# Local deformable attention: dense weights by one read per tile and one write per head, values by quarters, tokens loaded two chunks ahead

## The chip, the cores and the metric

The kernel runs on one core of a Trainium2 chip. The metric is the device time of one execution in microseconds (us). A core has TensorE (PE, whose weight loads are shown as PEld), VectorE (DVE), ScalarE (ACT) and GpSimd (POOL), and SyncE (SP), which issues transfers (DMAs); in this kernel ACT issues some too. Each engine runs its own instructions in the order in which they were put on its queue, and waits at an instruction until what it needs has come. L750 is line 750 of the kernel before.

## The reference, cut to what matters

The program is four layers; the change touches the first one's convolution. For every pixel of a 64 x 64 image, nine taps of four head groups (dilations 1, 3, 5, 7) are moved by learned offsets; keys and values are sampled there bilinearly, weighted by a mask, and attended over the nine taps.

```python
qkv = x @ w_qkv + b_qkv
qkv = conv2d(qkv.transpose(0, 3, 1, 2), w_dw, padding=1, groups=3 * c) + b_dw[None, :, None, None]
...
mask = jax.nn.sigmoid(conv1x1(pconv(q_img, pconv_mask_w), w_mask, b_mask))
for i in range(G):
    off = conv1x1(pconv(q_img, pconv_off_w[i]), w_off[i], b_off[i])
    dil = 2 * i + 1
    k_list.append(deform_sample(kv[0, :, i], off, mask, dil, dil * PAD))
    v_list.append(deform_sample(kv[1, :, i], off, mask, dil, dil * PAD))
...
attn = jax.nn.softmax(jnp.einsum('bgnc,bgckn->bgnk', qf, ks_), axis=-1)
out = jnp.einsum('bgnk,bgckn->bgnc', attn, vs_)
out = out.transpose(0, 2, 1, 3).reshape(b, h, w, c)
return out @ w_proj + b_proj
```

The layer adds its input to this: x + conv(norm(x)).

## The kernel before

`deformable_project` computes queries, keys, values and offsets of the four images (batches) and stores them to DRAM (qd, kd, vd, od). Where no offset is larger than one pixel, `deformable_near` does the rest. It needs no gather: every sample lies within one pixel of its tap, so a sample is a sum over a 3 x 3 neighbourhood with bilinear "hat" weights.

The near stage works on tiles of 128 pixels (two image rows), 32 to a batch, 128 in all; four tiles are a chunk, 32 chunks. A loop over T goes through the tiles, and the second half of a tile's work comes LAG = 14 tiles after the first. For tile or chunk:

- *Products* (`product`, L750): PE multiplies the tile's queries, laid out on POOL (qm, L721), with a band of keys from kpad, and ACT copies the result to `band` (`copy_products`, L760). band has two buffers per group, one chunk each.
- *Hats* (POOL, per chunk): from the offsets (of), `hats` makes the weights (L694 to L698), multiplies them by the mask (L702), and `hat_products` makes H, 3 x 3 weights of each tap (L708, four instructions of 324 elements). H has three buffers.
- *Attention* (DVE, per chunk, `attention`): within its tile a pixel's band starts at its own place; copies under a mask (`bit`) shift it there, first by one row (L768), then by 4, 2 and 1 columns (L771). Then band times H (L775), the sum (L782), the maximum, the exponential on ACT (L798), and `spread` (L799 to L818), which multiplies softmax weights and H into rows A.
- *Dense rows*: SP writes A to DRAM (`write`, L826: 16 transfers a chunk, one for each group and quarter of the partitions, since the row shift r is in the address), and every tile reads it back skewed (`read_dense`, L837: four transfers, two on SP, two on ACT), so that D holds a dense row of weights per pixel over a window of pixels. The DRAM buffers dd are zeroed once at the stage's start.
- *Values*: PE transposes D (L868), ACT copies to dt (L870), and PE multiplies with blocks of values (`weigh`, L888), each loaded by four transfers (`value_block`, L849).
- *Output* (per chunk): ACT copies the sum (oT, L900), SP loads the chunk's tokens xg (L904), POOL adds the bias (L905), PE projects (L911), ACT copies o (L913), POOL adds it to xg (L914), and SP stores the tokens (L920). xg has two buffers.

The order on PE is written out: `block` makes each of transpose, product, projection and weigh follow the one before (`issue_after`), and what stands in `behind` follows the last block. On the other engines a scheduler places the instructions by its own estimate of when they can run, so an engine's order may differ from the order of the calls; transfers are issued from the engine that the call names, in that engine's order.

## Time and profile before

| | |
|---|---|
| median of 3 runs | 7,705.08 us (7,700.91 to 7,719.4) |
| profiled execution | 7,690.3 us |
| its span | 7,688.3 us |
| mean granted TensorE clock | 0.892 |
| `deformable_project` | 0 to 671 us |
| near stage, start until the first steady chunks | 671 to 778 us |
| near stage, remainder | 778 to about 1,835 us |
| the other layers | about 1,835 to 7,688 us |

The page's 40 slices of 192 us each show the busy tenths of each engine; the near stage is in slices 4 to 9. The busy time of each engine by stage, in us:

| window | PE | PEld | DVE | ACT | POOL | clock | DMA share | GB/s |
|---|---|---|---|---|---|---|---|---|
| 0 to 671 | 566 | 251 | 123 | 209 | 8 | 0.94 | 0.44 | 105 |
| 671 to 778 | 51 | 38 | 68 | 16 | 81 | 0.66 | 0.72 | 218 |
| 778 to 1,835 | 788 | 661 | 669 | 357 | 392 | 0.83 | 0.71 | 201 |
| 1,835 to 7,688 | 5,117 | 2,592 | 3,961 | 2,109 | 1,261 | 0.90 | 0.12 | 32 |

### The profile page before, as it was taken

The numbers are of one execution on the slowest core, as the hardware profiler recorded it, in microseconds if no ns is written. First come the engines' busy times: TensorE is split into PE (matmuls) and PEld (weight loads), VectorE is DVE, ScalarE is ACT, GpSimd is POOL, SyncE is SP. The second block draws the span as 40 slices with busy tenths as digits, with TensorE's granted clock in tenths as the row PEclk, the third lists the DMA queues.
The fourth block names the chain that finished last, engine by engine and source line by source line (L and its number), as shares of the span: only waits on it lengthen the run. The fifth ranks groups of instructions, "written<-read, shape, count | busy, mean of one in ns | idle before, by whom it ended". The sixth has DMA issues, their size and how long they took to land. (4 is left out here: it accounts for less than half of the span.)

```text
span 7688.3 us, 157708 instructions
## 1 busy us (share of the span) xinstructions
PE 6522.7 (85%) x63791; PEld 3542.4 (46%) x63791; DVE 4821.5 (63%) x11178; ACT 2690.3 (35%) x6141; POOL 1741.4 (23%) x1634
## 2 busy tenths in 40 slices
PE   7995777775688868989989999798898997997989
PEld 3343666663455644345555555445225234242244
DVE  2113766764277554858856656674785875867877
ACT  3331333333234313611146555565104013031056
POOL 0003444320001100035532221154012112120135
PEclk9997887887799889999999988798897997988989
DMA  4436677775400022030100000001111111111101
GB/s 121 98 87 179 187 209 205 213 199 172 143 4 1 2 60 48 10 117 22 27 12 10 9 10 6 9 1 30 39 25 49 26 33 40 25 35 38 25 23 31
DMA packets 678781, 495.59 MB, mean 64 GB/s; under 512 B 302326, under 2 KB 594104, under 8 KB 674200
## 3 DMA queue, kind: packets, MB, share of 16 engines
q1 hardware_dynamic: 480910, 354.59, 17.0%
q10 hardware_dynamic: 197130, 130.77, 6.2%
q8 instruction: 509, 8.34, 0.5%
q14 instruction: 232, 1.90, 0.1%
HBM read 335.28 MB, written 149.75 MB: 63 GB/s over the span
## 5 line engine op out<-in xcount | busy, mean ns | idle before, releaser
L2476 DVE TENSOR_TENSOR t<-S,q 128x1536 f32<-128x1536 f32 (+3 forms) x608 | 1156.9, 1948 | 123.2 <-PE S L2464 117.9
L2464 PE MATMUL S<-R,L 32*128 32x512 f32 x4096 | 734.6, 651 | 90.3 <-DMA R<-wd 78.9
L2492 PE MATMUL acc<-t,sum 128*32 128x512 f32 x4096 | 639.5, 608 | 0.0
L750 PE MATMUL S<-kpad,qm 32*64 32x240 f32 (+3 forms) x8192 | 403.4, 421 | 216.0 <-ACT band L760 97.5
L2178 PE MATMUL pe<-ew,yT 128*128 128x512 f32 x1024 | 479.4, 603 | 27.4 <-DVE xs L2184 24.5
L1777 PE MATMUL acc<-w,attT 128*64 128x264 f32 x4096 | 486.3, 391 | 10.4 <-DVE w L1773 10.4
L2464 PEld LDWEIGHTS S<-R,L 32*128 32x128 f32 x4096 | 200.6, 186 | 611.4 <-issue 280.4
L2498 ACT COPY agg<-acc 128x512 f32<-128x512 f32 x32 | 18.8, 586 | 1194.0 <-DMA L<-pd 626.7
L750 PEld LDWEIGHTS S<-kpad,qm 32*64 32x64 f32 x8192 | 299.9, 156 | 271.5 <-issue 136.9
L1770 POOL TENSOR_TENSOR w<-xtl,ei 128x528 f32<-128x528 f32 x256 | 332.1, 1319 | 309.6 <-ACT ei L1769 204.5
L2184 DVE SCALAR_TENSOR_TENSOR xs<-pe,gate,xs 128x128 f32<-128x128 f32 x1024 | 332.5, 345 | 96.5 <-PE pe L2178 79.8
L1773 DVE TENSOR_TENSOR w<-xtl,pe 128x1056 f32<-128x1056 f32 x256 | 320.3, 1251 | 100.3 <-ACT ei L1769 89.4
L1777 PEld LDWEIGHTS acc<-w,attT 128*64 128x64 f32 x4096 | 284.0, 137 | 197.5 <-DVE w L1774 38.0
L2187 ACT ACTIVATE sc<-pe,gate 128x128 f32<-128x128 f32 x1024 | 291.3, 374 | 202.2 <-PE pe L2178 194.1
L514 PE MATMUL dw<-pad,diag 32*32 32x512 f32 x6912 | 310.4, 614 | 12.9 <-issue 7.0
L2507 POOL TENSOR_TENSOR o<-o,bf 128x512 f32<-128x512 f32 x32 | 40.7, 1271 | 1229.4 <-ACT o L2506 1229.4
L760 ACT COPY band<-S 128x144 f32<-128x144 f32 (+3 forms) x512 | 136.0, 351 | 480.4 <-DMA D<-dd 152.3
L2492 PEld LDWEIGHTS acc<-t,sum 128*32 128x32 f32 x4096 | 92.7, 108 | 458.4 <-issue 436.1
L2178 PEld LDWEIGHTS pe<-ew,yT 128*128 128x128 f32 x1024 | 185.6, 193 | 234.3 <-issue 151.4
L768 DVE COPY_PREDICATED band<-bit,band 128x432 f32<-128x432 int32 (+3 forms) x128 | 107.5, 895 | 270.0 <-ACT band L760 264.2
L868 PE MATMUL pt<-ident,D 128*128 128x128 f32 x1536 | 243.0, 315 | 29.2 <-DMA D<-dd 15.2
L771 DVE COPY_PREDICATED band<-bit,band 128x288 f32<-128x288 int32 (+11 forms) x384 | 243.0, 742 | 0.0
(520 smaller groups left out, 13065.8 us busy)
## 6 DMA issues: line engine op xcount, KB each, us to landing
vb<-vd SPq DMA_DIRECT2D x272, 256.0 KB
D<-dd ACTq DMA_DIRECT2D x128, 192.0 KB
D<-dd SPq DMA_DIRECT2D x128, 168.0 KB
D<-dd ACTq DMA_DIRECT2D x128, 144.0 KB
w<-in_e_weight_dram ACTq DMA_DIRECT2D x16, 1024.0 KB
w<-in_e_weight_dram SPq DMA_DIRECT2D x16, 1024.0 KB
wd<-s SPq DMA_DIRECT2D x32, 512.0 KB
D<-dd SPq DMA_DIRECT2D x128, 120.0 KB
```

What stands on the lines that cost most here:

```text
L514: nc.tensor.matmul(acc[g][32 * c : 32 * c + 32], diag[r, j, tap, :], pads[j][r, y0 : y0 + 8, tx : tx + 64], start=(tap == 0), stop=(tap == 8),
L750: ins = nc.tensor.matmul(acc[g][64 * h : 64 * h + 64].rearrange("p (a s) c -> p a s c", a=3), qm[rows, h, m, :], keys, start=(m == 0), sto ...
L771: nc.vector.copy_predicated(rows(0, [[CW[g], 3], [1, n]]), bit[:, :, :, i : i + 1].to_broadcast([128, 12, 3, n]), rows(s, [[CW[g], 3], [1, ...
L1770: nc.gpsimd.tensor_tensor(w2[:, 2:4], xt[:, 2:4, 0:2], window(ei, 0, [[0, 2], [0, 2], [1, 132]]), op=ALU.mult)
L1773: nc.vector.tensor_tensor(w1, xt[:, :, 1:3], window(pe, 0, [[0, 4], [0, 2], [1, 132]]), op=ALU.mult)
L1777: nc.tensor.matmul(acc[b // 2][64 * (b % 2) : 64 * (b % 2) + 64], attT[:, b // 2, hp, 64 * (b % 2) : 64 * (b % 2) + 64], src[:, b].rearran ...
L2178: nc.tensor.matmul(pe[h].rearrange("p e c -> p (e c)"), yT[:, 128 * t : 128 * t + 128], ew[:, 4 * h : 4 * h + 4, :].rearrange("p e c -> p ...
L2184: nc.vector.scalar_tensor_tensor(xt, pe[0][:, e, :], gate[:, t, e : e + 1], xt, op0=ALU.mult, op1=ALU.add)
L2187: nc.scalar.activation(sc[:, e, j, :], pe[1][:, e, :], AF.Copy, scale=gate[:, t, 4 + e : 5 + e])
L2464: nc.tensor.matmul(S[:, j, :], Ls[n % 2][r, ag, :], Rs[n % 2][r, ag].rearrange("p x y -> p (x y)"), start=True, stop=True)
L2476: nc.vector.tensor_tensor(t[:, j0:j1].rearrange("p u (x y) -> p u x y", x=8), S[:, j0:j1].rearrange("p u (x y) -> p u x y", x=8), qf[:, q0 ...
L2492: nc.tensor.matmul(acc[0][32 * h : 32 * h + 32, :], sum4, t[:, j, :], start=(u < 4), stop=(u >= 60))
```

## The change

- The dense rows: one buffer dd per chunk (three in turn) holds all four groups, with a row of 4 x 4 x 384 elements and 12 more (before: a buffer per group, of 240 to 384 elements a tile). `write` makes one transfer per group, four a chunk; `read_dense` one per tile, all on SP, and it covers the full 384 elements of each group.
- The row shift r is no longer in the address: hats along y have four rows instead of three, and `rows_of_hats` puts a pixel's three weights into rows 0 to 2 or 1 to 3 by its bit (`row`). So H, prod and t0 have 12 elements a tap instead of 9, A is filled over four rows, and the copies under a mask by one row (L768) are left out; those by 4, 2 and 1 columns run over all 48 rows. H has two buffers instead of three, dt three instead of four.
- The zero fill: three buffers, each by four transfers of 768 KB and a small one, all on ACT; only one tile of D is set to zero first.
- Values: `deformable_project` copies the values of each batch from vd into vq, rearranged by quarters (four transfers from DRAM to DRAM on SP). `value_block` is then one transfer.
- Offsets, queries, keys and tokens are loaded by ACT instead of SP. The tokens' load is called at the second tile of a chunk's last part, instead of after its fourth. Bias and tokens are added behind the projection's copy, next to the add of o.
- The hats are called three tiles earlier and the H products one; the offsets' loads three. A store is called two tiles after its add at the earliest.

In the changed program as it is built, these instructions stand so on POOL and ACT (steady part, one chunk, in order; a slash separates):

- POOL: add of o (chunk c) / add of the bias (chunk c+2) / two query copies / two H products / half a query copy / H / half a query copy / H / hats (four instructions) / their rows (seven) / a query copy / add of o (chunk c+1).
- ACT: tokens' load (chunk c+2) / band copies of the last tile of a chunk / dt / band copies / dt / exp / band copies / queries' load / oT / dt / offsets' load / band copies / copy of o / dt / tokens' load (chunk c+3).
- SP, per chunk: four writes of A / values / read of D / store of tokens / read of D / values / two reads of D.

```diff
+        vq = [dr.tile([32, 84, 4, 128], F32, tag=f"vq{b}", name=f"vq{b}") for b in range(4)]
...
+            for q in range(4):
+                nc.sync.dma_start(vq[b][:, :, q, :], vd[b][16 * q : 16 * q + 32])
...
-    PP = [12 * (15 + w) for w in W]
+    ROW = 4 * 4 * 384 + 12
...
+        row = wp.tile([128, 1], F32, tag="row", name="row")
+        nc.vector.tensor_copy(row, bit[:, 0, 0, 3:4])
...
-        dd = [[dr.tile([128, 4 * PP[g] + 12], F32, tag=f"dd{i}{g}", name=f"dd{i}{g}") for g in range(4)] for i in range(2)]
+        dd = [dr.tile([128, ROW], F32, tag=f"dd{i}", name=f"dd{i}") for i in range(3)]
 
         dense = [wp.tile([128, 4, 384], F32, tag=f"D{i}", name=f"D{i}") for i in range(4)]
-        for t in dense:
-            nc.gpsimd.memset(t, 0.0)
-        for i in range(2):
-            for g in range(4):
-                zero = dense[g].rearrange("p t n -> p (t n)")
-                eng = (nc.sync, nc.scalar)[g % 2]
-                eng.dma_start(dd[i][g][:, 0 : 4 * PP[g]], zero[:, 0 : 4 * PP[g]])
-                eng.dma_start(dd[i][g][:, 4 * PP[g] : 4 * PP[g] + 12], zero[:, 0:12])
-        Hs, bands, outs, vblocks, logits, ofs, hat_of, queries = {}, {}, {}, {}, {}, {}, {}, {}
-        accs, lefts, project, stores = {}, {}, [], []
-        last = [None]
+        nc.gpsimd.memset(dense[0], 0.0)
+        zero = dense[0].rearrange("p g n -> p (g n)")
+        for d in dd:
+            for t in range(4):
+                nc.scalar.dma_start(d[:, 1536 * t : 1536 * t + 1536], zero)
+            nc.scalar.dma_start(d[:, 6144:ROW], zero[:, 0:12])
+        Hs, bands, outs, vblocks, logits, ofs, hat_of, hy_of, queries = {}, {}, {}, {}, {}, {}, {}, {}, {}
+        accs, lefts, inputs, project, stores = {}, {}, {}, [], []
+        last, now = [None], [0]
...
-            nc.sync.dma_start(ofs[c], od[b][:, 4 * c8 : 4 * c8 + 4, :])
+            nc.scalar.dma_start(ofs[c], od[b][:, 4 * c8 : 4 * c8 + 4, :])
...
-            of = ofs.pop(c)
+            of = ofs[c]
...
-            mk = sm.tile([128, 3, 4, 3], F32, tag="mk", name="mk")
-            nc.gpsimd.tensor_copy(mk, window(of, 72, [[3, 3], [81, 4], [1, 3]]))
+        def rows_of_hats(c):
+            of, hat = ofs.pop(c), hat_of[c]
+            mk = sm.tile([128, 2, 36], F32, tag="mk", name="mk")
+            at = lambda i: window(mk, 36 * i, [[0, 4], [1, 36], [0, 3]])
+            nc.gpsimd.tensor_copy(mk[:, 0].rearrange("p (a t n) -> p a t n", a=3, t=4), window(of, 72, [[3, 3], [81, 4], [1, 3]]))
+            nc.gpsimd.tensor_scalar(mk[:, 1], mk[:, 0], row, None, op0=ALU.mult)
+            nc.gpsimd.tensor_tensor(mk[:, 0], mk[:, 0], mk[:, 1], op=ALU.subtract)
             hy = hat[:, 0:4].rearrange("p s a t n i -> p s (a t n) i")
-            nc.gpsimd.tensor_tensor(hy, hy, window(mk, 0, [[0, 4], [1, 36], [0, 3]]), op=ALU.mult)
-            Hs[c] = sm.tile([128, 4, 36, 9], F32, tag="H", name="H", bufs=3)
+            h4 = hy_of[c] = sm.tile([128, 4, 36, 4], F32, tag="hy", name="hy", bufs=1)
+            nc.gpsimd.tensor_tensor(h4[:, :, :, 0:3], hy, at(0), op=ALU.mult)
+            nc.gpsimd.tensor_tensor(hy, hy, at(1), op=ALU.mult)
+            nc.gpsimd.tensor_tensor(h4[:, :, :, 1:3], h4[:, :, :, 1:3], hy[:, :, :, 0:2], op=ALU.add)
+            nc.gpsimd.tensor_copy(h4[:, :, :, 3], hy[:, :, :, 2])
 
         def hat_products(c, groups):
-            H, hat = Hs[c], hat_of[c]
+            if 0 in groups:
+                Hs[c] = sm.tile([128, 4, 36, 12], F32, tag="H", name="H")
+            H, hat, h4 = Hs[c], hat_of[c], hy_of[c]
             for g in groups:
                 nc.gpsimd.tensor_tensor(
-                    H[:, g].rearrange("p n (a c) -> p n a c", a=3), window(hat, 108 * g, [[3, 36], [1, 3], [0, 3]]),
-                    window(hat, 108 * (4 + g), [[3, 36], [0, 3], [1, 3]]), op=ALU.mult,
+                    H[:, g].rearrange("p n (a c) -> p n a c", a=4), window(h4, 144 * g, [[4, 36], [1, 4], [0, 3]]),
+                    window(hat, 108 * (4 + g), [[3, 36], [0, 4], [1, 3]]), op=ALU.mult,
...
-            nc.sync.dma_start(
+            nc.scalar.dma_start(
...
-            nc.sync.dma_start(queries[n], qd[b].rearrange("p (y x) -> p y x", x=64)[:, 8 * h : 8 * h + 8, :])
+            nc.scalar.dma_start(queries[n], qd[b].rearrange("p (y x) -> p y x", x=64)[:, 8 * h : 8 * h + 8, :])
...
-            prod = sm.tile([128, 4, 36, 9], F32, tag="prod", name="prod", bufs=1)
+            prod = sm.tile([128, 4, 36, 12], F32, tag="prod", name="prod", bufs=1)
...
-                rows = lambda off, dims: window(band[g], off, [[4 * CW[g], 12]] + dims)
-                n = 3 * CW[g]
-                nc.vector.copy_predicated(rows(0, [[1, n]]), bit[:, 0, :, 3:4].to_broadcast([128, 12, n]), rows(CW[g], [[1, n]]))
+                flat = band[g].rearrange("p a t s c -> p (a t s) c")
                 for i, s in enumerate((4, 2, 1)):
                     n = W[g] + s - 1
-                    nc.vector.copy_predicated(
-                        rows(0, [[CW[g], 3], [1, n]]), bit[:, :, :, i : i + 1].to_broadcast([128, 12, 3, n]), rows(s, [[CW[g], 3], [1, n]])
-                    )
+                    nc.vector.copy_predicated(flat[:, :, 0:n], bit[:, 0, :, i : i + 1].to_broadcast([128, 48, n]), flat[:, :, s : s + n])
                 for tx in range(3):
                     nc.vector.tensor_tensor(
-                        window(prod, 324 * g + 9 * tx, [[27, 12], [3, 3], [1, 3]]),
-                        window(band[g], DIL[g] * tx, [[4 * CW[g], 12], [CW[g], 3], [1, 3]]),
-                        window(H, 324 * g + 9 * tx, [[27, 12], [3, 3], [1, 3]]), op=ALU.mult,
+                        window(prod, 432 * g + 12 * tx, [[36, 12], [3, 4], [1, 3]]),
+                        window(band[g], DIL[g] * tx, [[4 * CW[g], 12], [CW[g], 4], [1, 3]]),
+                        window(H, 432 * g + 12 * tx, [[36, 12], [3, 4], [1, 3]]), op=ALU.mult,
...
-                        window(A[g], ty, [[12 * DIL[g], 12], [3, 3], [12, 3]]), window(H, 324 * g + 108 * ty, [[9, 12], [3, 3], [1, 3]]),
-                        window(lg, 36 * g + 12 * ty, [[1, 12], [0, 3], [0, 3]]), op=ALU.mult,
+                        window(A[g], ty, [[12 * DIL[g], 12], [3, 4], [12, 3]]), window(H, 432 * g + 144 * ty, [[12, 12], [3, 4], [1, 3]]),
+                        window(lg, 36 * g + 12 * ty, [[1, 12], [0, 4], [0, 3]]), op=ALU.mult,
...
-            t0 = sm.tile([128, 36, 9], F32, tag="t0", name="t0", bufs=1)
-            nc.vector.tensor_tensor(t0, H[:, 0], window(lg, 0, [[1, 36], [0, 9]]), op=ALU.mult)
+            t0 = sm.tile([128, 36, 12], F32, tag="t0", name="t0", bufs=1)
+            nc.vector.tensor_tensor(t0, H[:, 0], window(lg, 0, [[1, 36], [0, 12]]), op=ALU.mult)
             for ty in range(3):
-                a0 = lambda m0, n: window(A[0], 12 * m0 + ty, [[60, 4], [12, n], [3, 3]])
-                tap = lambda tx, s0, n: window(t0, 108 * ty + 9 * tx + s0, [[27, 4], [1, n], [3, 3]])
+                a0 = lambda m0, n: window(A[0], 12 * m0 + ty, [[60, 4], [12, n], [3, 4]])
+                tap = lambda tx, s0, n: window(t0, 144 * ty + 12 * tx + s0, [[36, 4], [1, n], [3, 4]])
...
-            A = As[c % 2]
-            for g in (1, 2, 3, 0):
-                d, P = dd[c % 2][g], PP[g]
-                for j in range(4):
-                    r = j % 2
-                    nc.sync.dma_start(
-                        bass.AP(
-                            d.tensor, d.offset + 32 * j * (4 * P + 12) + 3 * r, [[4 * P + 12, 32], [P, 4], [1, 12 * W[g]]]
-                        ),
-                        A[g][32 * j : 32 * j + 32, :, 0 : W[g]].rearrange("p t c s a -> p t (c s a)"),
-                    )
+            for g, d in enumerate(DIL):
+                m = dd[c % 3]
+                nc.sync.dma_start(
+                    bass.AP(m.tensor, m.offset + 384 * g + 12 * (7 - d), [[ROW, 128], [1536, 4], [1, 12 * W[g]]]),
+                    As[c % 2][g][:, :, 0 : W[g]].rearrange("p t c s a -> p t (c s a)"),
+                )
 
         def read_dense(T):
             c, t = divmod(T, 4)
-            for g, d in enumerate(DIL):
-                m, P = dd[c % 2][g], PP[g]
-                (nc.sync, nc.scalar)[g % 2].dma_start(
-                    dense[t][:, g, 12 * (7 - d) : 12 * (7 - d) + P],
-                    bass.AP(m.tensor, m.offset + t * P, [[16 * (4 * P + 12), 8], [4 * P, 16], [1, P]]),
-                )
+            m = dd[c % 3]
+            nc.sync.dma_start(
+                dense[t].rearrange("p g n -> p (g n)"), bass.AP(m.tensor, m.offset + 1536 * t, [[16 * ROW, 8], [ROW - 12, 16], [1, 1536]])
+            )
...
-            d = vd[b]
-            for q in range(4):
-                nc.sync.dma_start(
-                    t[:, q].rearrange("p s c -> p (s c)"),
-                    bass.AP(d.tensor, d.offset + 16 * q * 10752 + 4 * kb * 128, [[10752, 32], [128, 4], [1, 512]]),
-                )
+            d = vq[b]
+            nc.sync.dma_start(
+                t.rearrange("p s q c -> p (s q c)"), bass.AP(d.tensor, d.offset + 4 * kb * 512, [[84 * 512, 32], [512, 4], [1, 2048]])
+            )
...
+            if T % 4 == 1:
+                inputs[0] = sm.tile([128, 4, 128], F32, tag="xg", name="xg")
+                nc.scalar.dma_start(inputs[0], tokens(x, b, i - 1, 4))
...
-                dt = sm.tile([128, 4, 128], F32, tag="dt", name="dt", bufs=4)
+                dt = sm.tile([128, 4, 128], F32, tag="dt", name="dt", bufs=3)
...
-                                quarter(outs[0][32 * g : 32 * g + 32, T % 4, :], q), vblocks[b, kb][:, q, si, 32 * g : 32 * g + 32],
+                                quarter(outs[0][32 * g : 32 * g + 32, T % 4, :], q), vblocks[b, kb][:, si, q, 32 * g : 32 * g + 32],
...
-                xg = sm.tile([128, 4, 128], F32, tag="xg", name="xg")
-                nc.sync.dma_start(xg, tokens(x, b, 4 * c, 4))
-                nc.gpsimd.tensor_tensor(xg, xg, bpj.to_broadcast([128, 4, 128]), op=ALU.add)
+                xg = inputs[0]
...
+            nc.gpsimd.tensor_tensor(xg, xg, bpj.to_broadcast([128, 4, 128]), op=ALU.add)
...
-            stores.append((b, c, xg))
+            stores.append((now[0], b, c, xg))
...
-        def store():
-            for b, c, xg in stores:
+        def store(some):
+            for o in some:
+                _, b, c, xg = o
                 nc.sync.dma_start(tokens(y, b, 4 * c, 4), xg)
-            stores.clear()
+                stores.remove(o)
...
+        offsets(1)
         products(0)
+        hats(0)
+        rows_of_hats(0)
         for T in range(128 + LAG):
+            now[0] = T
             with behind():
                 step(T, -1, products)
-                step(T, -2, offsets, 4)
-                step(T, 0, hats, 4)
-                step(T, 1, lambda c: hat_products(c, (0, 1)), 4)
-                step(T, 2, lambda c: hat_products(c, (2, 3)), 4)
+                step(T, -5, offsets, 4)
+                step(T, 0, lambda c: hat_products(c, (0, 1)), 4)
+                step(T, 1, lambda c: hat_products(c, (2, 3)), 4)
+                step(T, -2, hats, 4)
+                step(T, -1, rows_of_hats, 4)
...
-            late = list(stores)
+            late = [o for o in stores if o[0] <= T - 2]
...
-                if late:
-                    store()
+                store(late)
```

More of the change, by code (lines that the diff above doesn't have):

```diff
@@ L386, in stage_deformable @@
         od = [dr.tile([128, 32, 81], F32, tag=f"od{b}", name=f"od{b}") for b in range(4)]
-        far = deformable_project(k, fp, x, qd, kd, vd, od, w_qkv, b_qkv, w_dw, b_dw, pconv, w_offT, b_off)
+        vq = [dr.tile([32, 84, 4, 128], F32, tag=f"vq{b}", name=f"vq{b}") for b in range(4)]
+        far = deformable_project(k, fp, x, qd, kd, vd, vq, od, w_qkv, b_qkv, w_dw, b_dw, pconv, w_offT, b_off)
         with tc.If(far > 0) as branch:
@@ L390, in stage_deformable, with deformable_project @@
         with branch.Else():
-            deformable_near(k, dr, x, y, qd, kd, vd, od, masks, w_proj, b_proj)
-def deformable_project(k, fp, x, qd, kd, vd, od, w_qkv, b_qkv, w_dw, b_dw, pconv, w_offT, b_off):
+            deformable_near(k, dr, x, y, qd, kd, vq, od, masks, w_proj, b_proj)
+def deformable_project(k, fp, x, qd, kd, vd, vq, od, w_qkv, b_qkv, w_dw, b_dw, pconv, w_offT, b_off):
     nc, tc = k.nc, k.tc
@@ L606, in deformable_project, with deformable_near @@
         return nc.values_load(ei[0:1, 0:1], min_val=0, max_val=1)
-def deformable_near(k, dr, x, y, qd, kd, vd, od, masks, w_proj, b_proj):
+def deformable_near(k, dr, x, y, qd, kd, vq, od, masks, w_proj, b_proj):
     nc, tc = k.nc, k.tc
@@ L969, in deformable_near @@
             block(projection, *project.pop())
-        store()
+        store(list(stores))
 def prep_conv0(w):
```

## The prediction

> **What bounds the kernel now.** I read the slices first: the stage that is changed fills slices 4 to 9, from 671 us to about 1,835. Its middle, 800 to 1,700 us, was asked for by window.
>
> ```profile
> 800.00:1700.00 900.00, 680.31 (x18053) 568.32 (x18052) 599.99 (x1498) 301.82 (x809) 361.70 (x512) 0.83 0.73 206
> ```
>
> After the two lengths come PE, PEld, DVE, ACT, POOL, the granted clock, the DMA share and GB/s. No engine is full: PE 76%, DVE 67%, the 16 DMA engines 73%. So something goes round in a loop. The waits of the same window name two loops (total us, times, longest):
>
> ```profile
> POOL xg L905 <- DMA xg<-in_x_dram: 307.5, 18, 23.2
> DVE band L768 <- ACT band L760: 211.3, 25, 11.9
> ACT band L760 <- DMA D<-dd: 145.6, 28, 8.3
> PE S L750 <- ACT band L760: 88.1, 39, 5.7
> DVE m L799 <- ACT lg L798: 74.5, 26, 6.4
> ```
>
> POOL loses 17.1 us at a time for the tokens' load, DVE 8.4 us for band copies. The timeline of one chunk (four tiles) shows how the first one closes; start, length, engine, line, idle time before:
>
> ```profile
> 1201.48 1.28 POOL L914 TENSOR_TENSOR xg<-xg,o 128x512 f32<-128x512 f32 x1
> ...
> 1202.79 0.38 SPq L920 DMA_DIRECT2D x<-xg  x1
> ...
> 1203.22 5.02 SPq L826 DMA_DIRECT2D dd<-A  x7
> ...
> 1211.30 4.53 SPq L849 DMA_DIRECT2D vb<-vd  x4
> ...
> 1218.27 0.46 SPq L904 DMA_DIRECT2D xg<-in_x_dram  x1
> ...
> 1223.68 1.34 POOL L905 TENSOR_TENSOR xg<-xg,bpj 128x512 f32<-128x512 f32 x1 [16.64 <-DMA xg<-in_x_dram]
> ...
> 1226.42 3.15 POOL L708 TENSOR_TENSOR H<-hat 128x324 f32<-128x324 f32 x4 [1.19 <-DVE t L811]
> ...
> 1235.18 1.29 POOL L914 TENSOR_TENSOR xg<-xg,o 128x512 f32<-128x512 f32 x1
> ```
>
> L914 to L914 is 33.70 us here; from the first steady one (820.40) to the 27th (1,708.79) it is 888.4 us, 26 rounds of 34.2. A round is L914 (1.3), the store's issue, 15.5 us of SP issuing other transfers until the load at 1,218.27, 5.4 until POOL's L905 starts, then 11.5 of POOL work up to the next L914 (L905, mask, H, hats, queries). DVE runs its own loop beside it: band copy, 14.7 us of attention (L768 at 1,203.11 to the end of L792 at 1,218.04), exp, 4.5 to the end of L811, H, query copy, product, band copy: some 27 us, shorter, hence its 8.4 of waiting. PE goes from one tile's transposes to the next in 5.0 us where nothing stops it (1,201.96 to 1,206.98), so 20 a chunk.
>
> **The change part by part.** *SP's long list.* Writes go from 16 to 4 a chunk, reads of D from 16 (8 on SP) to 4, value blocks from four transfers to one; queries, offsets, keys and the tokens' load move to ACT. At 5.02/7 = 0.72 us an issue, SP had some 36 x 0.7 = 25 us of issuing a chunk and keeps about 11 x 0.7 = 8. That alone would take the 15.5 us out of POOL's round.
>
> *The tokens' load on ACT.* This is the decisive step. In the changed program's order the load of chunk c+2's tokens (changed line L868) stands on ACT just ahead of the band copies of the last tile of a chunk, and it waits: xg has two buffers, so the load needs chunk c's store to have landed. The store needs POOL's add of chunk c, and that add stands, in POOL's order, behind the four H products and the hats of later chunks. H has two buffers now, so those products wait for a spread, which follows the exp, which follows attention, which waits for that same last band copy. Queued on ACT behind the waiting load are all band copies, the copies of transposes, exp and the queries' load; PE and DVE wait for these. Before, the same load waited on SP, where no band copy stood behind it, so the two loops ran side by side. Now they are one, in series. One round, each part from a row of before:
> - add L914 1.28; store from issue to landing 4.2; load's issue (L904) 0.46; first band copies 0.4 (L760, 1.07 for four).
> - attention: 14.9 less the four L768 (3.58, from their mean 895 ns) and plus a third more elements in the rest. Two L771 forms 288 apart in size (288 and 576) differ by 331 ns (475, 806), 1.15 ns an element; 48 instead of 36 rows add 1,776 elements, +2.0. The reduction (1.50 for 1,296 elements) takes a third more, +0.5; twelve products +0.45. Together 14.3.
> - exp 0.32 and handover 0.1; spread to its last use of H 4.45, with a third more elements 4.9.
> - H: 432 elements on POOL cost 0.98 (L702), four of them 3.9, and two query copies between them 0.42 each: 4.75.
> - hats L694 to L698: 1.38 + 1.14 + 0.70 + 0.62 = 3.84. The new rows: two of 0.98, one of 288 (0.70), one copy 0.4, three small ones of 0.3: 3.96. Queries 0.84.
>
> Sum: 1.28 + 4.2 + 0.46 + 0.4 + 14.3 + 0.42 + 4.9 + 4.75 + 3.84 + 3.96 + 0.84 = 39.35 us, against 34.2. The store's landing is not shown by a wait: at least 1.7 (0.38 for the issue, 256 KB at 206 GB/s), at most the 5.4 of the load of equal size; I take 4.2, nearer the load. Ten handovers between engines add 0 to 1.5, late D reads up to 1 more. The round lies between 36.8 and 43. Over 26 rounds: 26 x 5.15 = **+134 us** (+68 to +229).
>
> *DMA.* One tile's D is 768 KB against 624 before. The transfer records never show more than eight packets of these reads at once, though the value blocks' 2,048-byte ones reach sixteen. A 6,144-byte packet takes 238 ns there: 128 x 0.238 / 8 = 3.8 us a read, 15.2 a chunk; with the rest of the traffic on those eight engines about 28 us a chunk, under 39, so it is hidden. If the loop were gone, it would be the next bound.
>
> [...]
>
> *The start.* The zero fill grows from 5.1 to 9.4 MB and goes wholly to ACT, ahead of three of the keys' loads and the first band copies. Its end already holds ACT in before (first band copy 694.96). The window 671 to 750 moved 245 GB/s: 4.3 MB more is 17.7 us, and the last batch's rearranged values (5.5 MB) compete for up to 22 more. I take +24 (+5 to +40). The first chunks' longer DVE work, where DVE is 85% busy in 750 to 850: +5 (0 to 10).
>
> *The end.* Twelve writes fewer before the last reads, 12 x 0.72 = 8.6: -8 (-15 to +5).
>
> *Values by quarters.* Four copies from DRAM to DRAM per batch, 10,752 packets of 512 bytes. The page's first queue gives 43 ns a packet on average (17.0% of 16 x 7,688 us over 480,910); over 16 engines 29 us, at 27 ns (512-byte records) 18. They stand on SP behind the offsets' stores, where the next transfers of a batch come some 50 us later, so most is hidden. Without that cover three batches lose up to 29 each. No row shows a DRAM to DRAM copy; +6 (0 to 85), near the hidden end.
>
> **Sum.** 7,690.3 (the profiled execution; span 7,688.3) + 134 + 24 + 5 - 8 + 6 = 7,851. The median of the runs, 7,705.1, is 14.8 higher, so **7,866 us**.
>
> **Rivals.** *Forecast, 0.71:* the joined loop, 7,770 to 7,980.
> *Faster, 0.11:* the load never really waits, because POOL's add runs long before ACT arrives. Then DVE's loop alone sets the pace: 0.4 + 14.3 + 0.42 + 4.9 + 4.75 + 0.45 for a query copy + 3 for a product = 28.2, level with the eight DMA engines' 28. That is -6.0 x 26 = -156; with the other +27 and 14.8, 7,576. For it: 307.5 us of POOL's waiting is really removed. Against: the add stands behind H and hats of the same round. It decides once the store lands before dt of the preceding tile is copied, which would need the add some 9 us earlier in POOL's order.
> *Eight engines, 0.06:* the loop is shorter than I think (bare engine times and an early store), and the eight engines at 82% of full set 28/0.82 = 34.2 a chunk: the coalescing does nothing, 7,690 + 27 + 14.8 = 7,732. For it: the DMA share is 0.73 already. Against: the lower bound of the round is 36.8.
> *Copies in the way, 0.12:* the joined loop, and the quartering delays three batches by 29 each: 7,866 + 81 = 7,947. For it: PE is busy 142.39 of 155 us (92%) in the projection of the second batch. Against: the pause on SP.
>
> **How the numbers follow.** The forecast is the likeliest's, 7,866. The likeliest's own range is 7,770 to 7,980; stretched down to the eight engines' case it is 7,720 to 7,980 and leaves out the faster rival and some 0.05 above. A measurement can tell 0.3% (23 us) from no change. Faster: 0.11 and a little of the third, 0.12; within 0.3%: 0.03 (half of the third); slower: 0.85.
>
> **What would show it.** Right: POOL's adds 38 to 41 us apart; ACT's band copies idle on the tokens' store or load; DVE waiting some 12 us or more a chunk for them; SP mostly idle. Wrong: a pace near 28 with D reads as the wait of PE's transposes, or rounds under 34; or a projection that ends well after 671 us. The first band copy near 719 would confirm the start.

## The result, and the profile after

The changed kernel is slower: a median of 8,042.2 us (8,023.4 to 8,052.8, four runs) against 7,705.8 for the kernel before in the same comparison; ratio 1.0431, interval [1.0407, 1.0455]. The forecast was 7,866, range 7,720 to 7,980: the direction is right, the loss is 336 us where 161 were expected.

The profiled execution has a span of 8,021.4 us, 333.1 more than before. The middle of the near stage by window (the two lengths, then PE, PEld, DVE, ACT, POOL, clock, DMA share, GB/s):

```profile
900.00:1900.00 1000.00, 618.00 (x15363) 515.25 (x15370) 519.18 (x1205) 272.05 (x694) 356.44 (x564) 0.72 0.69 174
```

PE is down from 76% to 62% and DVE from 67% to 52%: PE and DVE wait more. The waits of the same window (total, times, longest):

```profile
POOL xg L920 <- DMA xg<-in_x_dram: 491.6, 23, 25.3
DVE band L787 <- ACT band L778: 456.0, 22, 28.7
ACT band L778 <- PE S L768: 267.8, 62, 11.9
...
POOL mk L710 <- DMA of<-od: 96.5, 22, 8.3
PE out L896 <- issue: 91.8, 28, 6.7
PEld S L768 <- issue: 89.2, 68, 6.0
ACT band L778 <- DMA x<-xg: 87.1, 10, 13.3
```

and the row of the tokens' load (ACT's wait ahead of it, min/median/max in ns):

```profile
L868 ACTq EVENT_SEMAPHORE  x22: 38/8244/12533, 928.5 to 1869.1; - x22
```

DVE loses 20.7 us at a time (8.4 before) to the band copies, and band copies on ACT wait for the tokens' store, x<-xg, which cost 4.1 us in all before (800 to 1,700 us). The row of the load shows the same wait where it stands: 8.2 us in the median round. The timeline of one round, from one add of o to the next:

```profile
1414.32 1.27 POOL L921 TENSOR_TENSOR xg<-xg,o 128x512 f32<-128x512 f32 x1
...
1415.62 0.36 SPq L928 DMA_DIRECT2D x<-xg  x1
...
1418.31 0.39 ACTq L868 DMA_DIRECT2D xg<-in_x_dram  x1
1418.74 1.07 ACT L778 COPY band<-S 128x144 f32<-128x144 f32 x4 [8.22 <-PE pt L876]
1419.05 3.54 DVE L787 COPY_PREDICATED band<-bit,band 128x384 f32<-128x384 int32 x6 [20.35 <-ACT band L778]
...
1433.76 0.31 DVE L806 TENSOR_TENSOR lg<-lg,me 128x144 f32<-128x144 f32 x1
...
1437.89 0.60 DVE L825 TENSOR_TENSOR t<-H,lg 128x432 f32<-128x432 f32 x1
1438.29 1.31 POOL L920 TENSOR_TENSOR xg<-xg,bpj 128x512 f32<-128x512 f32 x1 [22.70 <-DMA xg<-in_x_dram]
...
1440.27 1.83 POOL L726 TENSOR_TENSOR H<-hy,hat 128x432 f32<-128x432 f32 x2
...
1444.37 0.24 POOL L739 COPY qm<-q 128x64 f32<-128x64 f32 x1 [2.27 <-PE S L768]
...
1445.64 0.95 POOL L726 TENSOR_TENSOR H<-hy,hat 128x432 f32<-128x432 f32 x1
```

and, later in the same round, the end of POOL's part:

```profile
1458.99 0.22 POOL L710 COPY mk<-of 128x36 f32<-128x36 f32 x1 [5.02 <-DMA of<-od]
...
1460.34 1.26 POOL L921 TENSOR_TENSOR xg<-xg,o 128x512 f32<-128x512 f32 x1
```

This is the chain that the prediction drew: add, store, load on ACT, band copy, attention, spread, H, hats, the next add, each starting where the one before ends. The profile puts ACT's wait ahead of the band copy at 1,418.74 down to PE's transposes, but the load stands ahead of that copy in ACT's order, and it went out only at 1,418.31, 2.7 us after the store's issue. The parts, in us, of this round (46.0, longer than the mean of 43.9) and as the mean of 26:

| part of the round | predicted | this round | mean of 26 |
|---|---|---|---|
| add of o to the first masked copy on DVE | 6.34 | 4.73 | 5.1 |
| attention (to the end of L806) | 14.3 | 15.0 | 15.0 |
| exp and spread (to the end of L825) | 5.3 | 4.4 | 4.9 |
| H with its query copies | 4.75 | 8.1 | 6.4 |
| hats, their rows, queries | 8.64 | 13.75 | 12.4 |
| round | 39.35 | 46.0 | 43.9 |

From the first steady add (888.36 us) to the 27th (2,029.24) the mean round is 43.88; before it was 34.17. The 333.1 us split so: 68.0 up to the first add of o, 26 x 9.71 = 252.5 in the rounds, 12.6 behind the 27th. Of these 12.6 none stand in the near stage: from the 27th add to the last it is 120.1 us, 120.8 before. They stand in the layers behind it, which the change does not touch, and from the last add to the end the profiled executions of all the kernels here take 5,851 to 5,884 us (5,858.8 before, 5,872.0 changed), so they need no cause in the change.

Two parts miss the sum, and in both a load that ACT had issued came late. The bias add (L920) stands on POOL ahead of the next query copies and H; it waited until 1,438.29 for a load issued at 1,418.31, 20 us. The next product on PE needed those query copies, a later query copy (2.27 of waiting for PE at 1,444.37) needed that product, and the last H stands behind it: 3.4 us in this round, 1.7 in the mean. The mask copy (L710) waited 5.0 for the offsets, a mean of 4.4 in the 23 rounds that have such a copy.

### The profile page after: what moved, and what is told of

Read it like the earlier page. It is cut to its first block, busy times and chain, and to the rows that moved or that the text cites. A ratio compares the mean times of both kernels' runs of the same rounds, so it can differ in the third digit from the quotient of the medians.

```text
span 8021.4 us, 156368 instructions
## 1 busy us (share of the span) xinstructions
PE 6584.4 (82%) x63791; PEld 3594.9 (45%) x63791; DVE 4832.2 (60%) x11051; ACT 2704.5 (34%) x6141; POOL 1803.4 (22%) x1791
## 5 line engine op out<-in xcount | busy, mean ns | idle before, releaser
L768 PE MATMUL S<-kpad,qm 32*64 32x144 f32 (+3 forms) x8192 | 432.1, 453 | 419.8 <-POOL qm L739 231.4
L787 DVE COPY_PREDICATED band<-bit,band 128x384 f32<-128x384 int32 (+11 forms) x384 | 316.6, 939 | 639.2 <-ACT band L778 569.9
L768 PEld LDWEIGHTS S<-kpad,qm 32*64 32x64 f32 x8192 | 320.2, 169 | 481.2 <-POOL qm L739 248.7
L876 PE MATMUL pt<-ident,D 128*128 128x128 f32 x1536 | 275.6, 345 | 30.9 <-issue 19.8
L878 ACT COPY dt<-pt 128x512 f32<-128x512 f32 x384 | 209.5, 603 | 233.5 <-PE pt L876 208.1
```

The source lines that it names most:

```text
L768: ins = nc.tensor.matmul(acc[g][64 * h : 64 * h + 64].rearrange("p (a s) c -> p a s c", a=3), qm[rows, h, m, :], keys, start=(m == 0), sto ...
L787: nc.vector.copy_predicated(flat[:, :, 0:n], bit[:, 0, :, i : i + 1].to_broadcast([128, 48, n]), flat[:, :, s : s + n])
```

## The experiments

Each was run beside the kernel before on the same chip; ratios are to that. "Round" is the mean of 26 between the first and the 27th add of o. The experiments' line numbers differ a little from one another.

| run | time, us | ratio, interval | first add of o | round |
|---|---|---|---|---|
| before | 7,705.8 | | 820.4 | 34.17 |
| changed | 8,042.2 | 1.0431 [1.0407, 1.0455] | 888.4 | 43.88 |
| e1 | 8,040.0 | 1.0431 [1.0407, 1.0455] | 889.0 | 44.30 |
| e2 | 8,018.8 | 1.0410 [1.0380, 1.0439] | 896.4 | 43.27 |
| e3 | 7,855.8 | 1.0191 [1.0167, 1.0216] | 892.1 | 37.64 |
| e4 | 8,035.5 | 1.0427 [1.0403, 1.0451] | 877.4 | 45.24 |
| e5 | 7,791.6 | 1.0129 [1.0092, 1.0166] | 892.9 | 34.54 |
| e6 | 7,762.4 | 1.0071 [1.0047, 1.0095] | 880.2 | 34.70 |
| e7 | 7,951.1 | 1.0325 [1.0295, 1.0355] | 875.7 | 41.09 |
| e8 | 7,727.6 | 1.0027 [1.0014, 1.0041] | 821.9 | 34.87 |
| e9 | 7,791.6 | 1.0114 [1.0094, 1.0134] | 869.1 | 35.50 |
| e10 | 7,771.6 | 1.0097 [1.0077, 1.0116] | 862.4 | 35.05 |
| e11 | 7,773.9 | 1.0091 [1.0071, 1.0111] | 872.7 | 34.63 |
| e12 | 7,910.7 | 1.0276 [1.0259, 1.0294] | 890.2 | 39.25 |
| e13 | 7,777.6 | 1.0103 [1.0086, 1.0120] | 852.0 | 35.81 |
| e14 | 7,702.4 | 0.9994 [0.9981, 1.0007] | 822.9 | 34.03 |
| e16 | 7,971.4 | 1.0355 [1.0338, 1.0372] | 855.3 | 42.89 |
| e17 | 7,714.7 | 1.0022 [1.0012, 1.0032] | 820.3 | 34.28 |
| e18 | 7,742.8 | 1.0050 [1.0033, 1.0067] | 885.6 | 33.87 |
| e19 | 7,935.7 | 1.0311 [1.0294, 1.0328] | 880.3 | 40.71 |

### Is the loop joined by the tokens' load on ACT?

**e1, three token buffers.**

```diff
-                inputs[0] = sm.tile([128, 4, 128], F32, tag="xg", name="xg")
+                inputs[0] = sm.tile([128, 4, 128], F32, tag="xg", name="xg", bufs=3)
```

> The changed kernel with three buffers for the tokens (t0 shares prod's buffer to make room). Theory (the loop is joined by the tokens' load, which waits on ACT for the store of two chunks before): the load now waits for the store of three chunks before, a round earlier, so ACT is not held; the round falls from 43.9 us towards 34 to 38 and the time from 8,042 to 7,800 to 7,890. Rival (the D reads on eight engines, or DVE's and POOL's added elements, set the round): no change, above 8,000.

Nothing changed, as the rival said, but the run does not speak for the rival: the wait that it was to remove is still there. In its timeline:

```profile
1430.18 0.36 SPq L928 DMA_DIRECT2D x<-xg  x1
...
1432.43 0.39 ACTq L868 DMA_DIRECT2D xg<-in_x_dram  x1
1432.86 1.07 ACT L778 COPY band<-S 128x144 f32<-128x144 f32 x4 [9.03 <-DMA x<-xg]
```

In the program as it was built, the load at this place is now the one of a chunk later: the scheduler put each load as early as a buffer comes free, so with three buffers it waits for the same store as with two. The run only shows that a buffer more does not part them.

**e3, tokens' load on SP; e2, bias added to o; e5, both; e6, three offsets' buffers as well.**

```diff
-                nc.scalar.dma_start(inputs[0], tokens(x, b, i - 1, 4))
+                nc.sync.dma_start(inputs[0], tokens(x, b, i - 1, 4))
```

```diff
-            nc.gpsimd.tensor_tensor(xg, xg, bpj.to_broadcast([128, 4, 128]), op=ALU.add)
+            nc.gpsimd.tensor_tensor(o, o, bpj.to_broadcast([128, 4, 128]), op=ALU.add)
             nc.gpsimd.tensor_tensor(xg, xg, o, op=ALU.add)
```

```diff
-            ofs[c] = sm.tile([128, 4, 81], F32, tag="of", name="of")
+            ofs[c] = sm.tile([128, 4, 81], F32, tag="of", name="of", bufs=3)
```

> The changed kernel with the tokens' load issued by SP instead of ACT, at the same call. Theory: no band copy stands behind the wait for the store any more, so the loop is open: 7,800 to 7,900, with ACT idle for the store gone and SP waiting there instead. Rival (the load's late landing is what costs, wherever it is issued): above 8,000.

> The changed kernel with the bias added to o instead of to the loaded tokens, so that POOL no longer waits for the tokens' load at the start of a round (22.7 us in the round from 1,414 us). Theory: the query copies behind that wait, and so the last two H products, come earlier by about 3.4 us a round: 26 x 3.4 = 88, about 7,955. Rival (only ACT's wait for the store counts, POOL's wait is idle time anyway): no change, 8,042 within 25.

> The changed kernel with both: the tokens' load on SP and the bias added to o. Theory: with the loop open, POOL's wait for the tokens (375.5 us over 27 rounds with the load on SP alone) and the late query copies behind it are what is left; without them the round falls from 37.6 us to 33 to 35, about 7,856 - 26 x 3.5 = 7,765 (7,720 to 7,810). Rival (bias to o alone brought 23 us, it brings no more here): 7,830 to 7,860.

> As the one with tokens on SP and bias to o, and three buffers for the offsets, so that their load can go out a chunk earlier (t0 shares prod's buffer). Theory: the waits of the mask copy for the offsets' load (74.7 us over 23 rounds) go, 2 to 3 us a round, 50 to 80 us less than with tokens on SP and bias to o alone. Rival (POOL is no longer on the loop, its wait costs nothing): the same within 20.

e3 took 186 us off, its rounds 37.6; the wait for the store now stands on SP, where no band copy is behind it. Two waits, POOL's from 900 to 1,900 us and SP's from 900 to 1,750:

```profile
POOL xg L920 <- DMA xg<-in_x_dram: 375.5, 27, 20.1
```

```profile
SPq L868 <- DMA x<-xg: 103.0, 22, 9.0
```

e2 alone gave 23 us, not 88, and rounds that swing between 38 and 53: POOL's 22 us went into waits for the spread and for PE, and the longer store wait on ACT (168.8 us in 13 times, 87.1 in the changed kernel). With the load on SP, in e5, the same edit gave 64 us by the medians, within what was expected. e6 gave 29 more, not 50 to 80.

**e8, that one part alone in the kernel before**: tokens' load on ACT at a chunk's second tile, bias behind the projection.

```diff
+            if T % 4 == 1:
+                inputs[0] = sm.tile([128, 4, 128], F32, tag="xg", name="xg")
+                nc.scalar.dma_start(inputs[0], tokens(x, b, i - 1, 4))
...
-                xg = sm.tile([128, 4, 128], F32, tag="xg", name="xg")
-                nc.sync.dma_start(xg, tokens(x, b, 4 * c, 4))
-                nc.gpsimd.tensor_tensor(xg, xg, bpj.to_broadcast([128, 4, 128]), op=ALU.add)
+                xg = inputs[0]
```

> The kernel before with one part of the change alone: the tokens' load issued by ACT at the second tile of a chunk, the bias behind the projection. By the sum of the loop from the rows of before (add 1.3, store 2.7, load issue and band copy 0.9, attention 14.9, exp and spread 4.9, H and queries 4.1, hats 5.1, queries 0.8) a round is 34.7 against 34.2: theory 7,705 to 7,760, if the load lands in some 5 us among small packets as before. Rival (the placement on ACT alone makes the change slow, whatever the rest): above 7,840.

7,727.6, and rounds of 34.87 where the sum gave 34.7. The old round of 34.17 is only 0.5 from that sum, so the agreement shows little. The wait for the store is there, in the timeline of the run:

```profile
1249.06 0.47 SPq L922 DMA_DIRECT2D x<-xg  x1
...
1254.34 0.38 ACTq L863 DMA_DIRECT2D xg<-in_x_dram  x1
1254.76 1.07 ACT L760 COPY band<-S 128x144 f32<-128x144 f32 x4 [11.70 <-DMA x<-xg]
```

Part of the 11.70 is ACT's issuing of D reads, which the kernel before has on ACT too; at the load itself ACT was held some 5 us here. The place costs 21 us there. So the place on ACT is not slow by itself, and the rival is out; what it costs depends on how long the rest of the chain is.

**e19, the joined loop without late loads**: the load still on ACT, bias to o, three offsets' buffers.

> The changed kernel with the tokens' load still on ACT, but with the bias added to o and three buffers for the offsets: the joined loop without the two late loads. It tests the prediction's own sum: a round of 39.35 us plus 1.3 for the bias add that now stands on the loop, 40 to 41, time 7,930 to 7,970. Rival (the loop is longer by itself, and the late loads are not what the sum missed): rounds of 43 or more, 8,010 or more.

7,935.7 and rounds of 40.71, against 39.35 + 1.3 = 40.65. Most rounds are between 39.5 and 41. Neither the bias add nor the mask copy waits for a load any more. The medians of the parts are 6.8, 15.1, 4.5, 4.2 and 10.0 us in the order of the table, against 6.34, 14.3, 5.3, 4.75 and 8.64 + 1.3: each is within about 0.8 of its term, and that the total is met to 0.1 is luck, since the misses cancel. The sum of the loop was right but for the two loads.

e19 and e6 differ in one line alone, the engine that issues the tokens' load: 40.71 against 34.70 us a round, ratios of 1.0311 and 1.0071. In e6 the step from the add to the first masked copy is 0.3 us instead of 6.8; the other four parts stay within 0.2. So the store and the load, as links of ACT's chain, cost 6 us a round, and attention, spread, H and what follows on POOL remain.

### Why do loads that ACT issues land late?

**e12, the same bytes from SP in smaller packets.**

```diff
+            for g in range(4):
+                nc.sync.dma_start(
+                    dense[t][:, g, :], bass.AP(m.tensor, m.offset + 1536 * t + 384 * g, [[16 * ROW, 8], [ROW - 12, 16], [1, 384]])
+                )
...
+            for q in range(4):
+                nc.sync.dma_start(
+                    t[:, q].rearrange("p q c -> p (q c)"),
+                    bass.AP(d.tensor, d.offset + (4 * kb + q) * 512, [[84 * 512, 32], [512, 4], [1, 512]]),
+                )
```

> The changed kernel with each tile's D read by four transfers of 1,536-byte packets and each value block by four of 2,048-byte packets, the same bytes, still from SP. [...]

7,910.7 and rounds of 39.25, where the changed kernel has 8,042.2 and 43.88. One of its loads, in its timeline:

```profile
1408.27 0.41 ACTq L871 DMA_DIRECT2D xg<-in_x_dram  x1
1408.72 1.07 ACT L778 COPY band<-S 128x144 f32<-128x144 f32 x4 [8.11 <-DMA x<-xg]
...
1417.41 4.90 POOL L923 TENSOR_TENSOR xg<-xg,bpj 128x512 f32<-128x512 f32 x1 [12.96 <-DMA xg<-in_x_dram]
```

From the issue of the load to the bias add that waits for it, 9.1 us; the median of the window's rounds is 9.1 too. In the changed kernel it is 19.5, before 5.9, and in e8, on ACT's queue beside SP's small packets, 3.9. In e3, on SP's queue and so behind or ahead of the same large packets, it is 8.1. So ACT's queue alone does not make it late, nor does the volume (e12 moves the same bytes), nor the large packets alone: it was late where the load stood on one queue and the large packets on the other. The mask copy's wait for the offsets, also a load of ACT's, fell with the packets in e12 too, from 4.4 to 0.4 us a round, and the rounds, 39.25, meet the sum of 39.35.

By the profile's records, one for each of what is called packets here, the load is 512 of 512 bytes, and the large ones beside it are of 6,144 and 8,192 bytes and last 374 and 500 ns on average there. In the changed kernel's round from 1,414 us the load's first record starts 6.65 us after its issue, half of the 512 have started at 9.3, and the last ends at 19.0; between the first and the last, 253 of the large ones on SP's queue start as well. How the DMA engines divide their time between the two queues was not shown. In e16, with the same queues and packet sizes, the median is 11.8 (8.9 to 21.8), so the two do not settle it alone; what else does was not taken apart.

### The start

**e4**, the zero fill on SP; **e16**, on the changed kernel, the fill and the keys' loads on SP, keys first, and the last batch's values rearranged in the middle of the stage. **e7**, **e9**, **e10** and **e13** vary the same on top of e6: two dense buffers and a fill issued in turn; keys and fill on SP; the last values later as well; keys ahead of the fill as well. The lines that differ:

```diff
-                nc.scalar.dma_start(d[:, 1536 * t : 1536 * t + 1536], zero)
+                nc.sync.dma_start(d[:, 1536 * t : 1536 * t + 1536], zero)
...
-            nc.scalar.dma_start(
+            nc.sync.dma_start(
                 kpad[:, 8 + 16 * h : 24 + 16 * h, 8:72], kd[b].rearrange("p (y x) -> p y x", x=64)[:, 16 * h : 16 * h + 16, :]
...
-            for q in range(4):
+            for q in range(4 if b < 3 else 0):
...
+            if T in (1, 2, 3):
+                with behind():
+                    for t in range(4):
+                        nc.sync.dma_start(dd[T - 1][:, 1536 * t : 1536 * t + 1536], zero)
...
-        dd = [dr.tile([128, ROW], F32, tag=f"dd{i}", name=f"dd{i}") for i in range(3)]
+        dd = [dr.tile([128, ROW], F32, tag=f"dd{i}", name=f"dd{i}") for i in range(2)]
```

> The changed kernel with the zero fill issued by SP instead of ACT. Theory: ACT, which is held 77.5 us by issues ahead of its first band copy at 740.73 us, reaches that copy some 25 to 45 us earlier, near 700 to 715, and the time falls by as much, to 8,000 to 8,015. Rival (the bytes of the fill, not who issues them, hold the start): no change, 8,042 within 10.

> The changed kernel as it is, with the start alone altered: keys' loads and fill on SP, keys first, the last batch's values rearranged later. It sizes the start's part of the loss: the first add of o comes from 888 to 835 to 850 us and the time falls by 35 to 60, to 7,980 to 8,010; the rounds stay at 42 to 45. Rival (what is gained at the start is lost again, since the keys' loads on SP disturb the rounds): 8,030 or more.

> As the one with three offsets' buffers, with two dense buffers in DRAM instead of three (6.3 MB of zeros instead of 9.4) and the fill issued by SP and ACT in turn. Theory: the first band copy comes from about 740 us to about 705 and 25 to 35 us of that are kept to the end. Rival (the first chunks wait for something else, as the fill on SP showed with 7 us): less than 10.

> As the one with three offsets' buffers (7,762), with the keys' loads and the zero fill issued by SP. What is left of its loss stands at the start: POOL's first add of o at 880.2 us against 820.4 before, the steady rounds being 34.7 against 34.2. Theory: ACT, held 76 us ahead of its first band copy by the fill's and the keys' issues, reaches it near 705 instead of 743; 25 to 40 us are gained, 7,720 to 7,740. Rival (bytes ahead of the keys, whoever issues): 7,750 or more.

> As the one with keys and fill on SP, and the last batch's values rearranged in the middle of the near stage instead of at its start. Theory: the 5.5 MB copied there hold SP's first loads (9 to 15 us from the end of the projection) and compete with the keys; 10 to 20 us less, 7,700 to 7,725, level with before. Rival: the same within 10 us.

> As the one with the last values later (7,772; first add of o 862 us), with the zero fill called in the loop, so that SP issues the four keys' loads ahead of it. Theory (the start is held by bytes ahead of the keys: the engines are 0.85 to 0.99 busy from 671 to 730 us there and the first product waits 53.9 us for the keys): the first product comes from 722.8 to under 700, the first add of o near 835, the time 7,735 to 7,755. Rival (the first chunks' own work sets it): first add of o above 855, 7,765 or more.

e4 brought the first band copy from 740.7 to 721.4 and the first add 11 us earlier, but 7 us at most in time, within the spread of the runs. e16 brought the first add to 855.3, 33 of the 68 us, and 71 us in all; its rounds are 1 us shorter too, where its loads on ACT landed sooner; why was not tested. On e6 the same steps bring the first add from 880.2 to 852.0, but the time does not follow (7,762 to 7,778): the rounds grow from 34.7 to 35.8, which takes the 28 us back. So bytes ahead of the keys are part of the start's loss (e10 and e13, by the first add of o), and what the rest is stays open.

e9, e10 and e13 missed the times that were expected. So did e7, but it taught something: with two dense buffers the rounds are 41.1. SP's own waits name it (900 to 1,750 us; 4.1 us in e6):

```profile
SPq L837 <- DMA D<-dd: 356.6, 28, 19.5
```

A write of A waits for the reads of the chunk two before; those are late, and SP's next reads, stores and values wait behind it. With these reads the third buffer is needed.

### What sets the kernel before at 34.2 us?

**e14**, bias added to o in the kernel before (the edit of e2); **e17**, three offsets' buffers as well.

> The kernel before with one line moved: the bias added to o behind the projection instead of to the loaded tokens. It tests what was said of the kernel before, that POOL's wait for the tokens' load sets its round of 34.2 us. Theory: POOL no longer waits for the load at the start of a round, only its last add needs it; DVE's loop of some 27 us or the eight engines' 26 to 28 set the pace, the round falls to 28 to 31 and the time by 80 to 150, to 7,550 to 7,625. Rival (POOL's wait was slack, something else sets 34 us): 7,680 to 7,710.

> The kernel before with the bias added to o and three buffers for the offsets, so that neither load that SP issues late in a chunk is needed by POOL in the same round. With the bias alone moved, POOL's wait went to the next load in SP's list (the mask copy waiting for the offsets: 313.6 us in 21 rounds, where the tokens' had been 307.5 in 18) and the time stayed. Theory (SP's list of some 25 us of issues a chunk, closed through POOL, sets 34.2 us): now the round falls to 29 to 32 and the time by 55 to 130, to 7,570 to 7,650. Rival (D reads on eight engines, with their issue on ACT ahead of band copies, set 34 us by themselves): 7,680 to 7,710.

No change in e14, and a loss of 0.2% in e17. In e14 POOL's wait went to the next load in SP's list:

```profile
POOL mk L700 <- DMA of<-od: 313.6, 21, 20.7
```

and in e17 to the spread:

```profile
POOL H L708 <- DVE t L811: 367.3, 25, 22.7
```

The first line is from 900 to 1,700 us, the second from 800 to 1,700. From 800 to 1,700 POOL's longest wait is 307.5 before, 356.7 in e14 and 367.3 in e17. POOL waits as long whatever it waits for, and the time stays. Its wait for the tokens was slack, and the prediction's reading of the kernel before was wrong. What sets the 34.2 stays open.

**e18**, reads of D over sixteen engines, on e6; **e11**, H with three buffers (six value blocks), on e10.

```diff
+                for t in range(4):
+                    nc.sync.dma_start(
+                        bass.AP(m.tensor, m.offset + 1536 * t + 384 * g + 12 * (7 - d), [[16 * ROW, 8], [ROW + 12, 16], [1, 12 * W[g]]]),
+                        As[c % 2][g][:, t, 0 : W[g]].rearrange("p c s a -> p (c s a)"),
+                    )
...
+                dense[t].rearrange("p g n -> p (g n)"), bass.AP(m.tensor, m.offset + 1536 * t, [[ROW, 128], [1, 1536]])
```

> As the one with tokens on SP, bias to o and three offsets' buffers (7,762; rounds of 34.7), with the skew moved from the read to the write: a tile's D is read from 128 rows at one stride, so the read can spread over sixteen engines; the writes become 16 a chunk, over eight. Theory (the D reads on eight engines set some 34 us a chunk in every version that has no other stall): the rounds fall to 28 to 32 and the time to 7,590 to 7,690, below before. Rival (the order of the engines' work, exp on ACT and the query copies among the H products, sets 34.7): 7,740 to 7,790.

> As the one with the last values later, with three buffers for H again (six for the value blocks make room). Theory: with ACT free, a round is attention, spread, H and the query copies that stand among the H products (34.7 us); with H not bound to the spread two chunks before, the round falls to 29 to 32 and the time by 70 to 140, below before. Rival (the eight engines of the D reads, about 28 us a chunk at full rate, hold at 34): the same within 20.

In e18 the records show up to sixteen and more of the read's packets at once (mostly eight in the changed kernel), and they last some 260 ns on average instead of 302 in e6; yet the rounds are 33.9, and the time is 20 us less than e6 by the medians, while the intervals overlap. e11 changed nothing. So neither the eight engines nor H's buffers hold the versions with the load on SP at 34 to 35. The waits of e18 point to the order of work:

```profile
POOL H L725 <- DVE t L824: 274.4, 23, 16.8
DVE band L786 <- ACT band L777: 174.7, 23, 9.5
ACT oT L908 <- POOL qm L738: 151.9, 23, 6.9
ACT lg L811 <- DVE lg L805: 139.2, 23, 9.9
```

ACT waits for attention's end at the exp, with band copies behind it; POOL waits for the spread at H, with query copies among them. No run altered that order, so this is argued only. No version beat the kernel before.

## Why the prediction was half right

- *The joined loop* was right, and shown: by the round's parts in the trace, by e3 (186 us back when the load leaves ACT), by e19 against e6 (that line alone, 40.71 against 34.70) and by the sums that e19 (40.71 against 40.65) and e12 (39.25 against 39.35) meet.
- *The step that failed* is "H ... 4.75" and "hats ... The new rows ... 3.96": both were sums of POOL's own instructions, with nothing for the loads that POOL waits for on the way. The prediction priced the load at its issue alone (0.46) and did not ask when it lands. In the changed kernel it took 19.5, its bias add stood ahead of the query copies and H, and the H part grew by 1.7 us in the mean of the rounds and the part of hats, rows and queries by 3.8, at the mask copy that waited for the offsets. The other three parts miss by 0.7, -0.4 and -1.2. Over 26 rounds 43.88 - 39.35 = 4.53 is 118 us of the 172 missed. e19 takes these two waits away and meets the sum; e12, which leaves the order as it is and cuts the packets beside the loads, meets it too.
- *Durations of single instructions* held: attention 15.0 for 14.3, H 0.94 for 0.98, the rows without their wait 8.73 for 8.64, the store's landing 2.4 in the changed kernel (median, from the store's issue to that of the load) and 4.7 in e19, for 4.2.
- *The start* was 68 us, not 24 + 5 + 6. The sum counted bytes, and would have had the first band copy near 719. It came at 740.73, after 77.5 us without work on ACT, 34.8 before:

```profile
694.96 1.07 ACT L760 COPY band<-S 128x144 f32<-128x144 f32 x4 [34.77 <-DMA dd<-D]
740.73 0.28 ACT L778 COPY band<-S 128x144 f32<-128x144 f32 x1 [77.53 <-issue]
```

  The issues of the fill and of three of the keys' loads fill 50 of the 77.5 us, from 690.57 on, and the DMA engines are 0.98 and 1.01 busy from 671 to 700 and 700 to 730 us. e16 won 33 of the 68. 33 us of the 172 stand here; what they consist of was not shown.
- *The end* of the near stage, from the 27th add to the last, was 0.7 us shorter, not 8: 7 of the 172. The last 13 are those of the layers behind, within what they vary by.
- *The D reads on eight engines* were rightly left off the path: e18 spreads them and gains 20 us by the medians. Their packets were mis-sized, 374 ns in the changed kernel for 238, an estimated 6.0 us a read for 3.8; and "never more than eight" is too strong for the kernel before, where its records show 10 to 13 at moments.
- *Shown wrong, but without weight in the sum:* that POOL's wait for the tokens sets the round before (e14, e17). The sum used the measured 34.2, whatever sets it.
- *The rivals:* the loop that stays open did not come, since the wait is real, and its 28 us would not have come either: the versions with the load on SP run at 34 to 35. Copies in the way of the projection cost little: the last batch's offsets leave for DRAM 3 us later than before.

## What to carry to other kernels

Moving a transfer's issue to a computing engine moved its waits too (ACT was held 8.2 us for the store in the median round here): look for what the transfer waits on, and follow from there whether the chain comes back to the same engine. Price each load on that chain from issue to landing beside the transfers that will run with it, not those that ran with it before: here the merged transfers had packets of 6,144 and 8,192 bytes, up to 2,048 before, and beside them a load in 512-byte packets on another queue took 19.5 us, 9.1 when they were cut to 1,536 and 2,048 (e12). A long idle time at an engine's wait is no proof that the wait sets the pace (307.5 us before; without it 356.7 at another load in e14, and the time the same); take it away and see whether it moves to the next instruction.

## What the runs showed of the hardware

A load of 256 KB in 512-byte packets took 5.9 us from issue to its user beside packets of up to 2,048 bytes on the same queue, 3.9 on the other queue beside such packets (e8), 19.5 on the other queue beside packets of 6,144 and 8,192 bytes, 8.1 on the same queue as these (e3), and 9.1 on the other queue when they were cut to 1,536 and 2,048 (e12; medians of the windows' rounds). With the large packets on the other queue it was not always late: 11.8 in e16. The packets of D's reads got shorter when the reads were spread over sixteen engines (302 ns in e6, some 260 in e18), and the kernel hardly gained.
